# Layer 1's attention with one joint query-key matrix: the normed input takes the place of the keys

## The chip, the cores and the metric

The kernel runs on one core of a Trainium2 chip. The metric is the device time of one execution in microseconds (us). The core has five engines that run side by side and wait for each other by semaphores: PE (TensorE, matmuls and transposes, which writes only to the accumulator memory, PSUM), DVE (VectorE), ACT (ScalarE), POOL (GpSimd) and SP, which issues most of the DMA transfers.

## The reference

The input x is 4 images of 256 channels and 32 x 32 = 1024 positions. Layer 0 is a block of state-space scans, convolutions and an eight-headed attention; it ends in x. Layer 1 treats the positions as tokens t of 256 channels: one attention with a single head of width 256, then a mixture of 16 experts of which each token uses two. All is in 32-bit floats. The part that the change touches:

```
t = _to_tokens(x)
t = t + _L1_attn_ref(_ln_t(t), Wq, bq, Wk, bk, Wv, bv)
t = t + _L1_ffn_ref(_ln_t(t), gate_w, gate_b, w1, w2, w3)

def _L1_attn_ref(traj, Wq, bq, Wk, bk, Wv, bv):
    q = jnp.einsum('bnd,ed->bne', traj, Wq) + bq
    k = jnp.einsum('bnd,ed->bne', traj, Wk) + bk
    v = jnp.einsum('bnd,ed->bne', traj, Wv) + bv
    scores = jnp.einsum('bnd,bmd->bnm', q, k)
    attn = jax.nn.softmax(scores, axis=-1)
    return jnp.einsum('bnm,bmd->bnd', attn, v)
```

A constant that is added to all scores of one query leaves the softmax as it is. With y for the normed token, the score of query n and key m is (Wq y_n + bq) . (Wk y_m + bk); the part with bk is such a constant, so y_m . (Wk^T Wq y_n + Wk^T bq) gives the same attention.

## The kernel before

The work is in stages along the time axis: layer 0's selective scan (about 0 to 1090 us), layer 0's attention for images 0 to 3, one after another (some 1160 to 2247 us), layer 1's attention for the same four images (about 2279 to 2726 us), and the experts with the final addition (to the end).

From layer 0's attention on, the order of every engine's instructions is not written out but computed, before the kernel is compiled, by the class `Plan`. Each step is handed to `add` with its engine, an assumed cost in ns, the keys of what it reads and writes, and the PSUM banks that it takes or gives back. `run` then picks, step by step, what can start first. There are three classes of steps. The main steps are the attention's tiles; each score tile carries a position (n in layer 0, 128 + i in layer 1). The side steps are given by `beside(first, last)`, which spreads the steps of a group evenly over the positions from first to last; such a step is not taken before its position is reached. The third class, low, holds the experts. There are four free PSUM banks (512 columns each); main steps may hold three of them at a time, side steps two, low steps one, and later two. A step that takes two banks waits until it can have both.

Side groups that matter here: `prepare` (line 939) runs in layer 0's attention for image 0, positions 4 to 20. It folds weights: `bias` (L947) multiplies a weight matrix by a bias column, `fold` (L955) multiplies two 256 x 256 matrices into two banks, and DVE copies the product back over the weight (L958). Beside it runs `ahead_of(1)` (line 983), which prepares image 1 for layer 0's attention, at positions 1 to 27. `after_of(b)` (line 1200) finishes layer 0 for an image; for the last one it runs at the start of layer 1's attention (convolution on DVE L1273, mean L1280).

`l1_before(b)` (line 1347) is layer 1's prologue for image b. For image 0 it is spread over positions 17 to 27 of layer 0's last image, for image b + 1 over five positions from the second score tile of image b. It subtracts the mean (`centred`, L1334 on PE, L1338 on DVE) into the buffer `ln`, normalises it in place (`normalised`: squares on ACT L1171, variance on PE L1176, roots on ACT L1182 and L1183, three DVE steps L1186 to L1192, and a multiply by POOL L1196), then projects queries and keys (`matmuls`, L936, evicted from PSUM by ACT with the bias, L1360), and values (L1371, evicted by DVE, L1375). The weights wq, wk and wv are loaded at the start of the kernel (L536).

`l1_attention(i)` (line 1380) handles tile i, 128 queries of image i // 8: scores against all 1024 keys (L1389), their maximum on DVE (L1392), exponentials on ACT (L1396), transposes of these (L1407), and, two tiles later, the weighted sum of the values (L1424). `l1_after(b, half)` (line 1442) runs for each half image: the second norm into the buffer `ln2`, logits of the router (L1458), the choice of two experts on DVE (L1472 to L1489), ranks (L1497) and the scatter of the routing table by POOL (L1531).

The buffers of all this have homes in a table, `homes` (L1315). A pair (s, j) is one of the four buffers of set s that layer 0's attention used; "e", "f", "g" are parts of the transposed exponentials' buffers. The experts later place their weights in set 0, set 1 and a scratch tile, and other things in "e" and "g".

Of the kernel before, what the change touches and what calls it, by code (L numbers as in the profile page):

```python
# [12 lines left out]
AF = mybir.ActivationFunctionType  # L13
# [7 lines left out]
P = 128  # L21
# [38 lines left out]
def _pack(i):  # L60

    f = {k.removeprefix("L0_conv_").removeprefix("L1_attn_").removeprefix("L1_ffn_"): np.asarray(v) for k, v in i.items()}
    f["skip_scale"] = np.asarray(i["L0_conv_skip_scale"])

    def ch(a):

        a = a.reshape(a.shape[0] // P, P, -1)
        return a.transpose(1, 0, 2).reshape(P, -1)

    def cols(a):  # L70

        return np.ascontiguousarray(a.reshape(a.shape[0] // P, P, -1).transpose(1, 0, 2))

    qdw_b = np.zeros((P, 1), np.float32)
    qdw_b[32 : 32 + NB, 0] = f["qdw_b"]
    vec = {
        "norm_w": ch(f["norm_w"]), "norm_b": ch(f["norm_b"]),
        "skip": np.broadcast_to(f["skip_scale"], (P, 1)),
        "qdw_b": qdw_b, "qpw_b": ch(np.repeat(f["qpw_b"], DM)),
        "rdw_w": ch(f["rdw_w"]), "rdw_b": ch(f["rdw_b"]), "rpw_b": ch(f["rpw_b"]),  # L80
        "fdw_w": ch(f["fdw_w"]), "fdw_b": ch(f["fdw_b"]), "fpw_b": ch(f["fpw_b"]),
        "lc_w": ch(f["lc_w"]), "lc_b": ch(f["lc_b"]), "inb": ch(f["attn_inb"]),
        "outb": ch(f["attn_outb"]), "lgn_w": ch(f["lgn_w"]), "lgn_b": ch(f["lgn_b"]),
        "fc_b": ch(f["fc_b"]), "dwc_w": ch(f["dwc_w"]), "dwc_b": ch(f["dwc_b"]),
        "proj_b": ch(f["proj_b"]), "bq": ch(f["bq"]), "bk": ch(f["bk"]),
        "convb": f["m_convb"].T,
        "dtb": f["m_dtb"].T, "dd": f["m_d"].T,

        "alog": f["m_alog"].reshape(NB, DIN // DB, DB, DS).transpose(3, 2, 0, 1).reshape(P, -1),
    }  # L90

    qdw, qpw = np.zeros((C, 3, 32), np.float32), np.zeros((3, 32, C), np.float32)
    for n in range(NB):
        qdw[n * DM : (n + 1) * DM, :, n] = f["qdw_w"][n]
    qpw[:, :NB] = np.repeat(f["qpw_w"][:, :, 0], DM, axis=0).T
    w = {
        "x": f["x"].reshape(B, C, N),
        "vec": np.concatenate([vec[n] for n, _ in _VEC], axis=1),
        "rows": np.concatenate([f["attn_inb"][2 * C :], f["bv"], f["gate_b"]])[None, :],
        "m_in": cols(f["m_inw"].transpose(0, 2, 1).reshape(NB * DM, 2 * DIN)),  # L100

        "convr": np.repeat(f["m_convw"].transpose(0, 2, 1).reshape(CT, 2, 1, K * DIN), DM, axis=2)
        .reshape(CT, P, K, DIN).transpose(1, 0, 2, 3),
        "m_xp": f["m_xpw"][:, :DTR].transpose(1, 0, 2),
        "m_bc": np.repeat(f["m_xpw"][:, DTR:], DB, axis=1).transpose(2, 0, 1),
        "m_dt": f["m_dtw"].transpose(2, 0, 1),
        "m_out": f["m_outw"].transpose(2, 0, 1),
        "qdw": cols(qdw.reshape(C, 96)),
        "qpw": qpw.reshape(96, C),
        "rpw": cols(f["rpw_w"][:, :, 0].T), "fpw": cols(f["fpw_w"][:, :, 0].T),  # L110
        "inw": cols(f["attn_inw"].T), "outw": cols(f["attn_outw"]),
        "fcw": cols(f["fc_w"].T), "projw": cols(f["proj_w"].T),
        "wq": cols(f["Wq"].T), "wk": cols(f["Wk"].T), "wv": cols(f["Wv"].T),
        "gw": cols(f["gate_w"]),

        "we": np.concatenate(
            [
                f[n].reshape(NE, f[n].shape[1] // P, P, -1).transpose(0, 2, 1, 3).reshape(NE * P, -1)
                for n in ("w1", "w2", "w3")
            ],  # L120
            axis=1,
        ),
    }

    strip = np.zeros((P, 2 * P - DB), np.float32)
    strip[np.arange(P), P - DB + np.arange(P) % DB] = 1.0

    pick = np.zeros((3, 32 // DB, DB, 32 // DB, DS, DB), np.float32)  # L130
    for j in range(32 // DB):
        for i in range(DB):
            pick[:, j, i, j, :, i] = 1.0
    grp = np.kron(np.eye(16, dtype=np.float32), np.full((8, 8), 1.0 / (8 * N), np.float32))
    w["const"] = np.concatenate(
        [
            np.eye(P, dtype=np.float32), grp, np.full((P, P), 1.0 / C, np.float32),
            np.broadcast_to(np.arange(NE, dtype=np.float32), (P, NE)),
            np.triu(np.ones((P, P), np.float32), 1), np.ones((P, P), np.float32),
            2.0 * np.arange(TT * P, dtype=np.float32).reshape(TT, P).T,  # L140
            np.broadcast_to(np.arange(NTILE, dtype=np.float32), (P, NTILE)),
            np.arange(P, dtype=np.float32)[:, None], strip,
        ],
        axis=1,
    )
    w["pick"] = pick.reshape(96, -1)
    return {k: np.ascontiguousarray(v) for k, v in w.items()}
# [169 lines left out]
def body(tc, g, out):  # L317
# [8 lines left out]
    with pool("const", 1) as cp, pool("dram", 1, space=bass.MemoryType.DRAM) as drp, contextlib.ExitStack() as late:  # L326
# [16 lines left out]
        def V(name, j=0, n=1):  # L343
            return vec[:, VOFF[name] + j : VOFF[name] + j + n]
# [530 lines left out]
        with pool("sets", 1) as wp, pool("work", 1) as kp, pool("ps2", 1, space=PSUM) as ps:  # L875
# [24 lines left out]
            rss = [kp.tile([P, CT, NT, 4], F32, tag=f"rs{i}", name=f"rs{i}") for i in range(2)]  # L900
            sts = [kp.tile([P, 4, CT], F32, tag=f"st{i}", name=f"st{i}") for i in range(2)]
            small = kp.tile([P, 16 + B * CT], F32, tag="small", name="small")
            fcb, projb, inbq, wmean, grb = small[:, 0:2], small[:, 2:4], small[:, 4:6], small[:, 8:12], small[:, 16:]
            S = [ps.tile([P, N], F32, tag=f"s{i}", name=f"s{i}") for i in range(2)]
            plan.banks = [ps.tile([P, 512], F32, tag=f"k{i}", name=f"k{i}") for i in range(4)]

# [32 lines left out]
            def prepare():  # L939
# [39 lines left out]
                add("DVE", 150, lambda: tt(projb, pb.t[:, 0:2], V("proj_b", 0, 2), ALU.add), (), ["projb"], pb, give=True)  # L979
                for k in range(CT):  # L980
                    add("DVE", 250, lambda k=k: ts(projw[:, k], projw[:, k], V("norm_w", k), None, ALU.mult), ["projw"], ["projw"])

            def ahead_of(b):

# [320 lines left out]
            def place(name):  # L1305
# [7 lines left out]
                return mid(s, j), lambda ks=range(CT), hs=range(2): BK(s, j, ks, hs)  # L1313

            homes = [  # L1315
                dict(ln=(0, 2), sq=(0, 1), q=(0, 3), k=(0, 1), v=(0, 0), ln2=(0, 2), sq2="e"),
                dict(ln=(1, 1), sq="f", q=(1, 3), k="f", v="g", ln2=(1, 1), sq2=(1, 0)),
                dict(ln=(0, 1), sq="e", q=(0, 3), k="e", v=(0, 0), ln2=(0, 1), sq2=(0, 2)),
                dict(ln=(1, 2), sq=(1, 0), q=(1, 3), k="f", v=(1, 0), ln2=(1, 2), sq2=(1, 1)),
            ]  # L1320
            homes = [{n: place(x) for n, x in home.items()} for home in homes]
            rows4 = prs[3].rearrange("p (t c) -> p t c", c=C)
# [24 lines left out]
            def l1_before(b):  # L1347

                home = homes[b]
                ln, lk = home["ln"]  # L1350
                centred([X[b][:, k] for k in range(CT)], lambda ks=range(CT), hs=range(2): KX(b, ks, hs), ln, lk, range(2))
                normalised(ln, lk, *home["sq"], prs[2], ("pr", 2), [range(2)])
                for what, w, bias in (("q", wq, "bq"), ("k", wk, "bk")):
                    dst, dk = home[what]
                    for m in range(CT):
                        for h in range(2):
                            bank = plan.bank()
                            matmuls(bank, w, m, ln, h, [lk([k], [h]) for k in range(CT)])
                            add(
                                "ACT", 580, lambda m=m, h=h, dst=dst, bias=bias, bank=bank: act(dst[m][:, HALVES[h]], bank.t, AF.Identity, bias=V(bias, m), scale=1.0),  # L1360
                                (), dk([m], [h]), bank, give=True,
                            )
                tile_v, vk = v_of(b)
                for u in range(NT // 2):
                    bank = plan.bank()

                    def value(u=u, bank=bank):
                        for c in range(2):
                            for k in range(CT):
                                tok = slice((2 * u + c) * P, (2 * u + c + 1) * P)  # L1370
                                mm(bank.t[:, c * C : (c + 1) * C], ln[k][:, tok], wv[:, k, :], start=k == 0, stop=k == CT - 1)  # L1371
                    add("PE", 1720, value, lk(hs=[u // 2]), (), bank, take=True)
                    dst = homes[b]["v"][0][u // 2][:, u % 2 * 2 * C : (u % 2 + 1) * 2 * C].rearrange("p (t c) -> p t c", c=C)
                    add(
                        "DVE", 690, lambda bank=bank, dst=dst: tt(  # L1375
                            dst, bank.t.rearrange("p (t c) -> p t c", c=C), rows[:, C : 2 * C].unsqueeze(1).to_broadcast([P, 2, C]), ALU.add
                        ), (), vk(2 * u), bank, give=True,
                    )

            def l1_attention(i):  # L1380


                if i < B * NT:
                    b, qt = i // NT, i % NT
                    (q, qk), (kk, kkeys) = homes[b]["q"], homes[b]["k"]
                    for h in range(2):
                        def scores(h=h):
                            for k in range(CT):
# [502 lines left out]
```

## Time and profile before

| what | value |
|---|---|
| median of three runs | 3217.78 us (3207.76 to 3220.32) |
| the profiled execution's own time | 3229.72 us |
| its span (first to last instruction) | 3227.9 us |
| granted clock of TensorE, mean | 0.940 |
| PE busy | 2862.9 us, 89% of the span |
| DVE, ACT, POOL busy | 2048.5, 1534.1, 1183.0 us |
| key projection on PE (L936, weight wk) | 64 records, mean 592 ns, 29.6 us busy |
| query projection on PE (L936, weight wq) | 64 records, mean 736 ns, 37.1 us busy |
| evictions of both (L1360, ACT) | 32, 687 ns each |

A busy share is the time in which an engine carries out at least one instruction. A matmul in 32-bit floats shows as two records, and records of successive matmuls overlap, so that busy time is less than count times mean. "idle before" names the engine whose signal ended a wait. Line numbers are those of the kernel before.

### The profile page before, as it was taken

The numbers are of one execution on the slowest core, as the hardware profiler recorded it, in microseconds if no ns is written. First come the engines' busy times: TensorE is split into PE (matmuls) and PEld (weight loads), VectorE is DVE, ScalarE is ACT, GpSimd is POOL, SyncE is SP. The second block draws the span as 40 slices with busy tenths as digits, with TensorE's granted clock in tenths as the row PEclk, the third lists the DMA queues.
The fourth block names the chain that finished last, engine by engine and source line by source line (L and its number), as shares of the span: only waits on it lengthen the run. The fifth ranks groups of instructions, "written<-read, shape, count | busy, mean of one in ns | idle before, by whom it ended". The sixth has DMA issues, their size and how long they took to land. (4 is left out here: it accounts for less than half of the span.)

```text
span 3227.9 us, 38992 instructions
## 1 busy us (share of the span) xinstructions
PE 2862.9 (89%) x15402; PEld 1616.7 (50%) x15402; DVE 2048.5 (63%) x2336; ACT 1534.1 (48%) x2102; POOL 1183.0 (37%) x747
## 2 busy tenths in 40 slices
PE   6788898988897689999899899988989999799997
PEld 3322222222222145565545555555545666689996
DVE  5899999999999646564865585585364445411112
ACT  3665666566565335455735754665433333211111
POOL 1677777777877400000000010001012123556662
PEclk8899999899999889999999899998989999899998
DMA  3666766676776400000000000000000002355455
GB/s 129 160 169 163 182 168 168 171 177 156 184 175 158 129 0 1 1 1 27 1 1 1 27 1 1 14 1 1 14 1 14 7 14 79 107 148 157 95 125 161
DMA packets 92872, 265.51 MB, mean 82 GB/s; under 512 B 18182, under 2 KB 36086, under 8 KB 89360
## 3 DMA queue, kind: packets, MB, share of 16 engines
q1 hardware_dynamic: 64000, 198.46, 23.2%
q0 software_dynamic: 26512, 60.35, 7.3%
q10 hardware_dynamic: 2176, 4.19, 0.3%
q8 instruction: 122, 2.00, 0.3%
q14 instruction: 62, 0.51, 0.1%
HBM read 291.70 MB, written 42.80 MB: 104 GB/s over the span
## 5 line engine op out<-in xcount | busy, mean ns | idle before, releaser
L841 POOL TENSOR_TENSOR hs<-hs,bc 128x1024 f32<-128x1024 f32 x256 | 603.0, 2357 | 252.1 <-DVE hs L840 235.9
L840 DVE TENSOR_TENSOR_SCAN hs<-dA,dBu 128x1024 f32<-128x1024 f32 x256 | 585.4, 2287 | 30.8 <-DVE dBu L837 1.9
L1106 DVE TENSOR_REDUCE nm<-s 128x1 f32<-128x1024 f32 x256 | 301.5, 1219 | 202.8 <-PE s L1101 201.7
L1111 ACT ACTIVATE pr<-s,nm 128x1024 f32<-128x1024 f32 x256 | 284.8, 1115 | 195.7 <-DVE nm L1106 193.8
L771 ACT ACTIVATE dA<-dA,aneg 128x1024 f32<-128x1024 f32 x256 | 288.9, 1145 | 157.9 <-DMA dA<-ds 148.3
L1125 PE MATMUL k<-const,pr 128*128 128x128 f32 x2048 | 302.1, 291 | 69.3 <-ACT pr L1111 48.3
L1196 POOL TENSOR_TENSOR b<-b,misc 128x1024 f32<-128x1024 f32 x16 | 36.4, 2295 | 892.2 <-DVE misc L1192 663.3
L1125 PEld LDWEIGHTS k<-const,pr 128*128 128x128 f32 x2048 | 234.7, 147 | 188.7 <-issue 82.7
L837 DVE TENSOR_TENSOR dBu<-dBu,bc 128x1024 f32<-128x1024 f32 x256 | 310.0, 1211 | 22.5 <-PE dBu L778 22.4
L1101 PE MATMUL s<-b,b 32*128 32x512 f32 x1024 | 287.7, 650 | 3.3 <-ACT pr L1111 3.3
L778 PE MATMUL dBu<-U,pick 96*128 96x512 bf16 x512 | 161.9, 399 | 123.6 <-DVE hs L840 123.4
L1131 ACT COPY pT<-k 128x512 f32<-128x512 f32 x320 | 175.6, 592 | 173.3 <-PE k L1125 172.2
L789 PE MATMUL pY<-hs,const 128*128 128x512 f32 x512 | 245.0, 601 | 10.8 <-DVE u L481 10.5
L1766 PE MATMUL s<-pT,b 128*128 128x128 f32 x1920 | 230.6, 276 | 3.5 <-DMA b<-we,intse 2.1
L1766 PEld LDWEIGHTS s<-pT,b 128*128 128x128 f32 x1920 | 226.7, 193 | 8.8 <-ACT pT L1769 3.6
L778 PEld LDWEIGHTS <-pick 96*128 96x128 bf16 x512 | 34.7, 98 | 325.9 <-DVE hs L840 206.0
L1770 DVE TENSOR_TENSOR pT<-pT,s 128x512 f32<-128x512 f32 x72 | 49.3, 685 | 229.2 <-ACT pT L1769 177.1
L1131 DVE COPY pT<-k 128x512 f32<-128x512 f32 x192 | 131.5, 686 | 98.8 <-PE k L1125 85.3
L1145 PE MATMUL k<-pT,b 128*32 128x128 f32 x4096 | 153.7, 292 | 17.2 <-DVE pT L1131 14.1
L1145 PEld LDWEIGHTS k<-pT,b 128*32 128x32 f32 x4096 | 114.1, 116 | 73.8 <-issue 30.8
L1101 PEld LDWEIGHTS s<-b,b 32*128 32x128 f32 x1024 | 102.9, 191 | 92.4 <-issue 77.4
L789 PEld LDWEIGHTS pY<-hs,const 128*128 128x128 f32 x512 | 96.5, 191 | 99.3 <-issue 82.3
(441 smaller groups left out, 4649.9 us busy)
## 6 DMA issues: line engine op xcount, KB each, us to landing
dA<-ds SPq DMA_DIRECT2D x256, 512.0 KB, 4.7
dq<-parts SPq DMA_DIRECT2D x15, 768.0 KB, 4.2
U<-dq SPq DMA_DIRECT2D x45, 256.0 KB, 6.0
ds<-dt SPq DMA_DIRECT2D x16, 512.0 KB, 3.0
b<-x SPq DMA_DIRECT2D x4, 1024.0 KB, 7.3
acc<-pr SPq DMA_DIRECT2D x8, 512.0 KB, 7.7
xm<-x SPq DMA_DIRECT2D x4, 1024.0 KB, 5.0
tokens<-pr SPq DMA_DIRECT2D x8, 512.0 KB, 2.9
```

The costliest lines, as they stand in the source:

```text
L771: act(dAs[t], dAs[t], AF.Exp, scale=aneg[:, c : c + 1])
L789: mm(r["pY"][:, h], strip[:, P - DB - j * DB : 2 * P - DB - j * DB], hs[:, h], start=p == 0, stop=p == NJ - 1)
L837: tt(dBu, dBu, r["B"], ALU.mult)
L840: nc.vector.tensor_tensor_scan(hs, dAs.pop(t), dBu, 0.0, ALU.mult, ALU.add)
L841: nc.gpsimd.tensor_tensor(hs, hs, r["C"], ALU.mult)
L1101: mm(S[i][:, HALVES[h]], qT[rr, qt * P : (qt + 1) * P], kT[rr, HALVES[h]], start=True, stop=True)
L1106: "DVE", 1220, lambda i=i, u=u: nc.vector.tensor_reduce(nms[u], S[i], AX.X, ALU.max, negate=True),
L1111: "ACT", 1330, lambda i=i, u=u, hd=hd: act(prs[u % 4], S[i], AF.Exp, bias=nms[u], scale=1.0, accum_out=rss[b % 2][:, k, qt, hd : hd + 1]), ...
L1125: nc.tensor.transpose(bank.t[:, j * P : (j + 1) * P], prs[u][:, c0 : c0 + P], ident)
L1131: lambda dst=dst, bank=bank, on_act=on_act: (nc.scalar.copy if on_act else nc.vector.tensor_copy)(dst, bank.t),
L1145: mm(bank.t[i * HD : (i + 1) * HD, 0:P], v[:, 4 * jh + j, hd * HD : (hd + 1) * HD], pTs[m][jh][:, i, j * P : (j + 1) * P], start=j == 0, s ...
L1766: mm(p12[:, a, c], wbufs[w][:, o : o + P], xT[:, k], start=k == 0, stop=k == CT - 1)
```

## The change

The host hands wq and wk over untransposed. `prepare` gets three steps more, behind its old ones: `q_bias` forms Wk^T bq (four matmuls of one column), `join` forms the joint matrix from wq and wk (four matmuls of 256 columns into two banks), and DVE copies both out of PSUM, the matrix over wq. In the prologue the query projection uses the joint matrix and the new bias; the key projection and its evictions are gone. The scores read `ln` where they read the keys. `ln` must then keep its content until the last score tile of its image, so `ln2`, which used to overwrite it, gets another home, and some homes are exchanged.

```diff
-        "wq": cols(f["Wq"].T), "wk": cols(f["Wk"].T), "wv": cols(f["Wv"].T),
+        "wq": cols(f["Wq"]), "wk": cols(f["Wk"]), "wv": cols(f["Wv"].T),
...
+                qb = plan.bank()
+
+                def q_bias():
+                    for m in range(CT):
+                        for k in range(CT):
+                            mm(qb.t[:, m : m + 1], wk[:, k, m * P : (m + 1) * P], V("bq", k), start=k == 0, stop=k == CT - 1)
+                add("PE", 600, q_bias, ["wq"], (), qb, take=True)
+                add("DVE", 150, lambda: nc.vector.tensor_copy(qbias, qb.t[:, 0:2]), (), ["qbias"], qb, give=True)
+                joint = [plan.bank() for _ in range(CT)]
+
+                def join():
+                    for i in range(CT):
+                        for k in range(CT):
+                            mm(joint[i].t[:, 0:C], wq[:, k, i * P : (i + 1) * P], wk[:, k, :], start=k == 0, stop=k == CT - 1)
+                add("PE", 1800, join, ["wq"], (), joint, take=True)
+                for i in range(CT):
+                    add("DVE", 400, lambda i=i: nc.vector.tensor_copy(wq[:, i], joint[i].t[:, 0:C]), (), ["wq"], joint[i], give=True)
...
-                dict(ln=(0, 2), sq=(0, 1), q=(0, 3), k=(0, 1), v=(0, 0), ln2=(0, 2), sq2="e"),
-                dict(ln=(1, 1), sq="f", q=(1, 3), k="f", v="g", ln2=(1, 1), sq2=(1, 0)),
-                dict(ln=(0, 1), sq="e", q=(0, 3), k="e", v=(0, 0), ln2=(0, 1), sq2=(0, 2)),
-                dict(ln=(1, 2), sq=(1, 0), q=(1, 3), k="f", v=(1, 0), ln2=(1, 2), sq2=(1, 1)),
+                dict(ln=(0, 2), sq=(0, 1), q=(0, 3), v=(0, 0), ln2=(0, 1), sq2="e"),
+                dict(ln=(1, 1), sq="f", q=(1, 3), v="g", ln2="f", sq2=(1, 0)),
+                dict(ln=(0, 2), sq="e", q=(0, 3), v=(0, 0), ln2="e", sq2=(0, 1)),
+                dict(ln=(1, 2), sq=(1, 0), q=(1, 3), v=(1, 0), ln2="f", sq2=(1, 1)),
...
-                for what, w, bias in (("q", wq, "bq"), ("k", wk, "bk")):
-                    dst, dk = home[what]
...
-                            matmuls(bank, w, m, ln, h, [lk([k], [h]) for k in range(CT)])
+                dst, dk = home["q"]
...
+                        matmuls(bank, wq, m, ln, h, [lk([k], [h]) + ["wq"] for k in range(CT)])
...
+                            "ACT", 580, lambda m=m, h=h, dst=dst, bank=bank: act(dst[m][:, HALVES[h]], bank.t, AF.Identity, bias=qbias[:, m : m + 1], scale=1.0),
+                            ["qbias"], dk([m], [h]), bank, give=True,
...
-                    (q, qk), (kk, kkeys) = homes[b]["q"], homes[b]["k"]
+                    (q, qk), (kk, kkeys) = homes[b]["q"], homes[b]["ln"]
```

More of the change, by code (lines that the diff above doesn't have):

```diff
@@ L902, in body @@
             small = kp.tile([P, 16 + B * CT], F32, tag="small", name="small")
-            fcb, projb, inbq, wmean, grb = small[:, 0:2], small[:, 2:4], small[:, 4:6], small[:, 8:12], small[:, 16:]
+            fcb, projb, inbq, qbias, wmean, grb = small[:, 0:2], small[:, 2:4], small[:, 4:6], small[:, 6:8], small[:, 8:12], small[:, 16:]
             S = [ps.tile([P, N], F32, tag=f"s{i}", name=f"s{i}") for i in range(2)]
@@ L1352, in l1_before @@
                 normalised(ln, lk, *home["sq"], prs[2], ("pr", 2), [range(2)])
-                for what, w, bias in (("q", wq, "bq"), ("k", wk, "bk")):
-                    dst, dk = home[what]
-                    for m in range(CT):
-                        for h in range(2):
-                            bank = plan.bank()
-                            matmuls(bank, w, m, ln, h, [lk([k], [h]) for k in range(CT)])
[L1359 to L1362, printed above, removed]
+                dst, dk = home["q"]
+                for m in range(CT):
+                    for h in range(2):
+                        bank = plan.bank()
+                        matmuls(bank, wq, m, ln, h, [lk([k], [h]) + ["wq"] for k in range(CT)])
+                        add(
+                            "ACT", 580, lambda m=m, h=h, dst=dst, bank=bank: act(dst[m][:, HALVES[h]], bank.t, AF.Identity, bias=qbias[:, m : m + 1], scale=1.0),
+                            ["qbias"], dk([m], [h]), bank, give=True,
+                        )
                 tile_v, vk = v_of(b)
```

## The prediction, made before the result was known

> **What bounds the kernel now.** I read the page's busy shares first, then the busy time by stretch of the span, then TensorE's waits in layer 1's attention, and last TensorE's own timeline where the removed work stands.
>
> The first two rows of the page say that TensorE (PE) is the fullest engine over the whole span and that it is nearly full in the second half (the right half of the digits, mostly 9).
>
> ```profile
> PE 2862.9 (89%) x15402; PEld 1616.7 (50%) x15402; DVE 2048.5 (63%) x2336; ACT 1534.1 (48%) x2102; POOL 1183.0 (37%) x747
> ...
> PE   6788898988897689999899899988989999799997
> ```
>
> A mean is not enough, since layer 0's scan (0 to 1090 us) has other limits. The busy times by stretch, cut at the borders of the batches, are these (columns: stretch, length, PE, weight loads, DVE, ACT, POOL, then granted clock):
>
> ```profile
> 1160.00:1457.00 297.00, 274.22 (x2153) 161.10 (x2153) 164.91 (x194) 154.24 (x279) 3.95 (x2) 0.95 0.00 1
> ...
> 2247.00:2279.00 32.00, 26.21 (x131) 15.55 (x130) 6.56 (x9) 9.76 (x15) 4.29 (x2) 0.89 0.00 1
> 2279.00:2361.00 82.00, 81.76 (x312) 50.16 (x311) 43.33 (x62) 36.21 (x51) 4.67 (x2) 1.00 0.04 13
> 2361.00:2395.00 34.00, 23.03 (x57) 11.20 (x58) 24.25 (x28) 16.48 (x19) 5.64 (x2) 0.82 0.00 0
> 2395.00:2425.00 30.00, 30.00 (x90) 16.68 (x88) 9.76 (x12) 7.25 (x10) 7.10 (x5) 0.92 0.00 1
> 2425.00:2508.00 83.00, 77.64 (x297) 48.71 (x298) 40.48 (x107) 28.48 (x43) 24.25 (x35) 0.96 0.05 14
> 2508.00:2621.00 113.00, 108.14 (x438) 70.50 (x437) 53.23 (x130) 38.80 (x58) 26.54 (x38) 0.98 0.03 10
> 2621.00:2726.00 105.00, 100.99 (x438) 68.72 (x437) 54.90 (x160) 34.62 (x53) 24.93 (x39) 1.00 0.11 26
> ```
>
> Layer 1's attention is the stretch from 2279 to about 2726 us. There PE is 94 to 100% busy, except for 34 us from 2361 to 2395; DVE and ACT are about half idle. It is bound by the amount of PE work, so PE work taken out of it should come off the time. In batch 0 of layer 0's attention (1160 to 1457) PE is 92% busy; work put there costs nearly its own length.
>
> The waits of PE from 2247 to 2726 us, in total, are short (columns: us in total, times, longest):
>
> ```profile
> PE k L1497 <- DVE rsum L1428: 8.9, 3, 4.4
> PE k L936 <- POOL b L1196: 5.9, 4, 2.5
> PE k L1280 <- DVE b L1273: 4.4, 1, 4.4
> ```
>
> The timeline of PE at the seam between the layers shows the removed work in place:
>
> ```profile
> 2257.98 7.24 PE L936 MATMUL k<-b,wq 128*128 128x512 f32 x14 [0.36 <-POOL b L1196]
> 2265.06 7.03 PE L936 MATMUL k<-b,wk 128*128 128x512 f32 x16
> 2271.93 7.07 PE L1371 MATMUL k<-wv,b 128*128 128x256 f32 x32
> 2278.83 1.88 PE L1389 MATMUL s<-b,b 128*128 128x512 f32 x4
> ```
>
> The key projection (wk) starts as soon as the query projection ends, and values and scores follow it without a gap. Nothing waits beside it: it is 2271.93 - 2265.06 = 6.87 us of the path.
>
> **What the Trainium skill says.** "Perfetto Trace Analysis", Identifying the Most-Contended Engine: busy matmul time is a poor measure of distance to the roofline because matmuls are pipelined. I use it only to see whether PE ever stands still, and take costs from start to start, not from mean duration: the 16 records of wk have a mean of 592 ns each, which would be 9.5 us, but take 6.87. "TensorE: Matmul & The Clock Gate", The HAM clock gate: PE falls to half clock after an idle window of about 3.4 us. The trace agrees: in the stretch with the 4.36 us wait the clock granted is 0.82, and a wq record that has a median of 592 ns takes up to 1222. "GPSIMD Engine Reference", Specifications: GpSimd shares SBUF interfaces with VectorE and contends with DVE instructions that have two SBUF inputs. The trace agrees: L1474, a subtraction of 64 columns, has a median of 225 ns and takes 2192 beside the POOL multiply of L1196.
>
> **The change part by part.**
>
> Durations of the nearest rows (the sources' own views; min/median/max):
>
> ```profile
> L936 PE MATMUL k<-b,wk x64: 590/592/595, 2265.1 to 2623.9; 128*128 128x512 f32 x64
> L947 PE MATMUL k<-vec,fcw x8: 250/250/271, 1206.6 to 1207.4; 128*128 128x1 f32 x8
> L955 PE MATMUL k<-fcw,outw x8: 379/379/483, 1239.5 to 1241.2; 128*128 128x256 f32 x8
> L958 DVE COPY fcw<-k x2: 415/416/417, 1242.7 to 1259.3; 128x256 f32<-128x256 f32 x2
> ```
>
> Removed from PE: the key projection, 8 matmuls of 512 columns (16 records) per batch, 6.87 us. In batch 0 it is one block; in batches 1 to 3 it is four pieces of 1.72 us (2410.03 to 2411.75 is one), again 6.87 us. PE shows no idle time from 2394 to 2425, nor from 2491 to 2525 and from 2605 to 2640 where the others stand. Sum 4 x 6.87 = 27.5 us, all on the path.
>
> Removed from ACT: 16 evictions (L1360, 687 ns) = 11.0 us. ACT is about half idle there, and scores come after the value projection, so they hid under PE. I count 0. Were ACT the bound they would be worth up to 11.0.
>
> Added to PE, once, in prepare during batch 0 of layer 0: the bias q_bias has the shapes of L947, from 1206.58 to the next instruction at 1207.50 = 0.92 us. The product join has the shapes of L955, 1239.54 to 1241.46 = 1.92 us. Sum 2.8 us. At 92% busy I count it in full; its bounds are 0 (it falls into the 18.3 us that PE waits there for ACT's exponentials, L1111) and about 5. The upper end is the hold of banks: side work may hold two of the four banks at a time and join takes both. Of its twin's two copies, one came at 1242.7 and one at 1259.3, so one bank was out for 17 us; in that time PE waited 0.79 + 0.79 us. So 2.8 plus about 2.
>
> Added to DVE: two copies of 416 ns and one of about 150 (L949, 148 ns) = 1.0 us, where DVE is busy 165 of 297 us. I count 0; without that cover it is 1.0.
>
> Waits that are added: the query matmuls wait for the new wq and their evictions for qbias. Both are made before about 1400 us and used from 2256 us, so behind them nothing stands. No DMA is issued, removed or moved; the key weights are loaded as before, and no instruction of SP or POOL is moved past another by hand.
>
> Moved: buffers. Batch 0's ln stays in its place until its eighth score tile (about 2355 us); its next owner is batch 2's ln, whose first mean is at 2433 us: 78 us to spare. Batch 1's ln place passes to batch 3's second-norm squares two batches later. The second norm takes places that the squares or the keys had. The experts wait for places "e", "g" and the whole of set 0, and these are last read by the second norm of batch 2 either way. I count 0, bounds 0 and 2 us.
>
> Moved: the plan. The order on every queue is computed from costs and positions, and layer 1's prologue now has 32 steps in place of 40 over the same five positions, so its POOL multiplies fall due about half a position later (5 x 15/32 - 5 x 15/40 = 0.47; batch 1's eight score tiles take from 2425.5 to 2536, 13.8 us each, so about 6 us). At 2256 and 2391 us the query projection waits for that multiply, which had been due long before; in batches 2 and 3 it stands two score tiles ahead of its own first scores (2491 against 2536 us). I count 0. What can move is the meeting of POOL's multiply with the routing steps of L1474 to L1489, which today costs PE the three waits of L1497, 8.9 us. A new plan can lose them (-8.9) or make one in each of the other five halves (5 x 4.4 = +22).
>
> What is late next: after the keys are gone, PE's own rest, 94 to 100% busy. In the 34 us from 2361 PE waits for the tail of batch 3 of layer 0 on DVE (L1273) and the normalisation chain. That chain starts at 2278 us (L1204), directly behind the value evictions, so it comes 6.87 us earlier with them, and the wait keeps its length.
>
> Sum: -27.5 + 2.8 = -24.7 us. The profiled execution took 3229.72 us (span 3227.9): 3205.0. It lies 11.94 us above the median of the three runs, 3217.78 (3207.76 to 3220.32), so in those terms 3193.1, or -0.77%.
>
> **The rivals.** About 0.5% (16 us) is what a measurement of this kernel can tell from no change.
>
> A, the forecast: all four projections come off, 3193. For it: no PE gap at any of them. Chance 0.60.
>
> B, only half comes off. If the tail chain at 2361 does not start earlier with the seam, batch 0's 6.87 us becomes wait there; and one more meeting with POOL eats about 4.4: -24.7 + 6.9 + 4.4 = -13.4, 3204. For it: that stretch is the one place where DVE's chain and not PE sets the end. Against it: the chain's first step stands right behind the value evictions. Chance 0.24.
>
> C, more comes off: the three L1497 waits go as well, -24.7 - 8.9 = -33.6, 3184. For it: two of them come from POOL's multiply starting in the very microsecond in which the routing steps start, and that multiply now falls due later. Chance 0.09.
>
> D, slower. Place: join in batch 0 of layer 0. While it waits for two free side banks and holds them, the preparation of batch 1 behind it stands still. Its last PE step today ends about 1393 us and batch 1 begins about 1457, so 64 us are spare. The hold decides only from there: to be slower by 16 us it would have to last 64 + 24.7 + 16 = 105 us. A hold of 110 us gives 3239. Against it: the twin held for 17 us. Chance 0.07.
>
> That the keys' work is not really removed can't be: scores read ln in place of k, and no other step makes k.
>
> **How the numbers follow.** Likeliest: 3193. A spreads by some 8 us, since three runs of one kernel spread over 12.6. Of A about 0.53 is beyond 16 us, with C's 0.09 and 0.04 of B: faster 0.66. Same: the rest of A and B, 0.27. Slower: 0.07. The range leaves out D and the outer tails: from 3177 (C less 7) to 3214 (B and 10 of spread).
>
> **What would show it.** Right: no wk rows; PE busy in all lower by about 25 us; the value projection directly behind the query projection at the seam; the distance from the first layer 1 score to the end of the last one shorter by about 20 us, with waits of PE as long as before. Two small groups for the join near 1200 to 1400 us. Wrong: the start of layer 1 later than before by more than 3 us (D or a worse plan of layer 0); longer waits of PE in 2247 to 2726, with L1497 or L936 <- POOL (B); or the wait at L1280 grown by 6.9 us.

## The result and the profile after

The changed kernel takes 3189.95 us (median of six runs, 3184.59 to 3197.09). Six runs of the kernel before give 3214.79 (3207.76 to 3220.32). The difference of the medians is 24.8 us. The ratio is 0.993, with a 95% interval of 0.9919 to 0.9942: 0.6 to 0.8% faster. The forecast was 3193.

The page of the kernel after shows PE with 39 us less to do than before. Its place as the fullest engine and the digits of the second half have hardly changed:

```profile
PE 2824.0 (89%) x15354; PEld 1598.7 (50%) x15354; DVE 2047.2 (64%) x2339; ACT 1522.3 (48%) x2086; POOL 1183.4 (37%) x747
...
PE   6788888898888779999899889989989999899996
```

The busy times by stretch, with PE's in the third column: image 0 of layer 0's attention; the seam up to the first score of layer 1; to the first score of image 1; to the first query projection of image 2; to that of image 3; to the last score. The last cuts lie earlier in their images than those of the prediction's table, so these rows can't be compared with that table one by one:

```profile
1160.00:1457.00 297.00, 271.43 (x2136) 158.66 (x2134) 164.75 (x196) 152.59 (x276) 3.95 (x2) 0.95 0.00 1
2242.00:2268.00 26.00, 20.12 (x119) 12.87 (x118) 6.33 (x9) 7.45 (x11) 4.29 (x2) 0.80 0.00 1
2268.00:2405.00 137.00, 125.96 (x432) 72.73 (x431) 76.25 (x102) 57.90 (x76) 17.60 (x9) 0.94 0.02 8
2405.00:2472.00 67.00, 62.76 (x266) 41.85 (x264) 37.99 (x94) 23.97 (x35) 15.50 (x20) 1.00 0.06 16
2472.00:2579.00 107.00, 102.14 (x425) 68.45 (x425) 53.50 (x134) 36.04 (x53) 26.54 (x38) 0.98 0.04 11
2579.00:2697.00 118.00, 111.44 (x464) 74.38 (x465) 57.29 (x171) 36.12 (x55) 34.68 (x55) 0.96 0.11 27
```

Over the whole of layer 1's attention with its seam, PE was busy 447.77 of 479 us before and is busy 422.42 of 455 now. So 25.4 us of work are gone, while the idle time stayed (31.2 and 32.6 us). The waits of PE in that window (us in total, times, longest) are the same ones with nearly the same lengths, except for one on a DMA:

```profile
PE k L1516 <- DVE rsum L1447: 8.5, 3, 4.0
PE k L936 <- POOL b L1216: 5.8, 3, 2.9
PE k L1708 <- DMA misc<-table,tcole: 5.5, 1, 5.5
PE k L1300 <- DVE b L1293: 4.4, 1, 4.4
```

(L1516, L1447, L1216, L1300 and L1293 are L1497, L1428, L1196, L1280 and L1273 of the kernel before.) L1708, L1689 before, belongs to the experts, which begin beside the last scores. In this profile of the kernel before PE waited there for only 1.2 us:

```profile
PE k L1689 <- DMA misc<-table,tcole: 1.2, 1, 1.2
```

In a second profile of the same kernel (before_again, below) it waited 5.3 us, so the longer wait is not the change's.

At the seam the timeline of PE shows what filled the removed block's place: the value projection now follows the query projection directly.

```profile
2251.90 9.80 PE L936 MATMUL k<-b,wq 128*128 128x512 f32 x16 [2.93 <-POOL b L1216]
2261.54 7.07 PE L1390 MATMUL k<-wv,b 128*128 128x256 f32 x32
2268.44 1.88 PE L1408 MATMUL s<-b 128*128 128x512 f32 x4
```

The added steps stand in layer 0's image 0, in order the bias product, the joint product and its two copies:

```profile
L990 PE MATMUL k<-vec,wk x8: 250/250/271, 1302.0 to 1302.8; 128*128 128x1 f32 x8
```

```profile
L998 PE MATMUL k<-wk,wq x8: 379/379/483, 1323.8 to 1325.4; 128*128 128x256 f32 x8
L1001 DVE COPY wq<-k x2: 414/415/416, 1330.0 to 1340.2; 128x256 f32<-128x256 f32 x2
```

The two first profiles differ by 43.1 us (spans of 3227.9 and 3184.8), which is more than the medians do. By stage, from the first score of layer 0 to the first query projection, from there to the start of the last score record of layer 1, and from there to the end of the span:

| kernel | layer 0's attention | layer 1's attention | experts and end |
|---|---|---|---|
| before | 1080.5 | 470.1 | 501.8 |
| after | 1075.9 | 444.5 | 488.4 |
| difference | -4.6 | -25.6 | -13.4 |

Only the middle column holds the removed work; of the change, the first holds the small added steps and the last nothing. The experiments look at the outer ones. Within the middle column, the time falls at every image (from the first query projection to the first score of image 0, then from first score to first score, then to the last score; before_again is the second profile of the kernel before):

| kernel | seam | image 0 | image 1 | image 2 | image 3 |
|---|---|---|---|---|---|
| before | 22.8 | 146.7 | 110.4 | 113.0 | 77.2 |
| before_again | 22.8 | 146.6 | 110.4 | 113.0 | 80.8 |
| after | 16.6 | 136.9 | 104.2 | 106.1 | 80.7 |

An image's projection runs beside the image ahead of it, so the four blocks lie in the first four columns, and each column lost 6 to 10 us. The last column holds the wait on the DMA.

### The profile page after: what moved, and what is told of

It reads as the page before. It is cut to its first block, busy times and chain, and to the rows that moved or that the text cites. A ratio compares the mean times of both kernels' runs of the same rounds, so it can differ in the third digit from the quotient of the medians.

```text
span 3184.8 us, 38887 instructions
## 1 busy us (share of the span) xinstructions
PE 2824.0 (89%) x15354; PEld 1598.7 (50%) x15354; DVE 2047.2 (64%) x2339; ACT 1522.3 (48%) x2086; POOL 1183.4 (37%) x747
## 5 line engine op out<-in xcount | busy, mean ns | idle before, releaser
L1216 POOL TENSOR_TENSOR b<-b,misc 128x1024 f32<-128x1024 f32 x16 | 36.4, 2299 | 887.5 <-DVE misc L1212 835.4
L837 DVE TENSOR_TENSOR dBu<-dBu,bc 128x1024 f32<-128x1024 f32 x256 | 310.0, 1211 | 19.9 <-PE dBu L778 19.8
```

What stands on the lines that cost most here:

```text
L837: tt(dBu, dBu, r["B"], ALU.mult)
```

## The experiments

**First question: is it the removed PE work, or something that went with it?** Three kernels add parts of the key projection back to the changed kernel as dead work, so their outputs are unchanged. `keys_back` adds all of it:

```diff
+                for m in range(CT):
+                    for h in range(2):
+                        bank = plan.bank()
+                        matmuls(bank, wk, m, ln, h, [lk([k], [h]) for k in range(CT)])
+                        add("ACT", 580, lambda m=m, bank=bank: act(kx, bank.t, AF.Identity, bias=V("bk", m), scale=1.0), (), ["kx"], bank, give=True)
```

> The changed kernel with the key projection added again as dead work: the same 8 matmuls of 512 columns per image with the key weights (32 in all) and the same 16 evictions by ACT, into a scratch tile that nobody reads; scores still read the normed input. Theory work (what counts is PE work taken from a full PE): all four projections cost their start-to-start time again, 4 x 6.87 = 27.5, so 3189.95 + 27.5 = 3217.5 us, about 2.7 slower than the kernel before (the join is still there). Theory plan (the gain came from a luckier order of the queues, since the whole plan is computed anew): the time stays near 3190 or lands anywhere, not at +27. Theory half (only the seam and one image's block count): about 3204.

`keys_pe_only` keeps the matmuls and gives the bank back without an eviction:

```diff
+                        matmuls(bank, wk, m, ln, h, [lk([k], [h]) for k in range(CT)])
+                        bank.ops[-1]["give"] = True
```

> The changed kernel with only the PE half of the key projection added again: 32 matmuls of 512 columns into a PSUM bank that is given back at once; no eviction, no ACT work. Theory work: 3217.5, the same as with evictions, since these hid under PE. Theory ACT (the evictions or the time for which a bank is held were what was removed): clearly less, at most half of the 27.5, 3204 or below.

`evict_only` adds only ACT instructions:

```diff
+                        add("ACT", 580, lambda m=m, h=h, dst=dst: act(kx, dst[m][:, HALVES[h]], AF.Identity, bias=V("bk", m), scale=1.0), dk([m], [h]), ["kx"])
```

> The changed kernel with 16 ACT instructions of 512 columns added, each a second pass over a query tile into a scratch tile that nobody reads, so ACT has as much to do as with the key evictions (16 x 0.687 = 11.0 us) and PE has no more. Theory work: within 2 us of 3190. Theory ACT: +11, 3201.

They ran on a chip where the kernel before takes 3227.13 us, so they are compared by ratio to it:

| kernel | median us | ratio to before | 95% interval |
|---|---|---|---|
| changed kernel (first measurement) | 3189.95 | 0.993 | 0.9919 to 0.9942 |
| keys_back | 3228.65 | 1.0008 | 0.9998 to 1.0018 |
| keys_pe_only | 3230.02 | 1.001 | 0.9998 to 1.0021 |
| evict_only | 3203.93 | 0.9924 | 0.9909 to 0.994 |

The matmuls alone bring back 1.001 / 0.993 = 0.8%, some 26 us of 3190; the two intervals together leave about 5 us either way. With the evictions it is no more. The evictions alone change nothing that can be measured. All three kernels keep the new homes of the buffers and an order that is computed anew, so neither of these is the gain either. It is the PE work, and ACT's 11 us hid under it. The profile of keys_pe_only has the key projection's 64 records, and layer 1's attention takes 474.1 us again (2258.3 to 2732.4):

```profile
L936 PE MATMUL k<-b,wk x64: 590/592/593, 2267.9 to 2622.1; 128*128 128x512 f32 x64
```

**Second question: what does the preparation cost?** `join_only` adds the new steps to the kernel before, with their results in scratch tiles:

```diff
+                add("PE", 600, q_bias, ["wq"], (), qb, take=True)
+                add("DVE", 150, lambda: nc.vector.tensor_copy(qbias, qb.t[:, 0:2]), (), ["qbias"], qb, give=True)
...
+                add("PE", 1800, join, ["wq"], (), joint, take=True)
+                for i in range(CT):
+                    add("DVE", 400, lambda i=i: nc.vector.tensor_copy(jt[:, i], joint[i].t[:, 0:C]), (), ["jt"], joint[i], give=True)
```

> The kernel before with only the new steps of the preparation added: the bias product, the joint product into two banks, and the three copies by DVE, into scratch tiles that nobody reads; queries and keys are projected as before. Theory work: +2.8 (bounds 0 and 5), 3217.6 against 3214.8. Theory plan: a shift of up to 10 us in either direction, since the plan of layer 0 is computed anew. Theory bank hold: +5 or more, with waits of PE between the join and its second copy.

Measured 3230.57, ratio 1.0011 (0.9998 to 1.0024): +3.5 us, with an interval from -0.6 to +7.7. The estimate of 2.8 lies within it, and so does nothing at all; the price is not settled more closely than that.

`join_one_bank` asks whether the two banks matter. On the changed kernel both halves go into one bank:

```diff
-                joint = [plan.bank() for _ in range(CT)]
+                joint = plan.bank()
...
-                            mm(joint[i].t[:, 0:C], wq[:, k, i * P : (i + 1) * P], wk[:, k, :], start=k == 0, stop=k == CT - 1)
+                            mm(joint.t[:, i * C : (i + 1) * C], wq[:, k, i * P : (i + 1) * P], wk[:, k, :], start=k == 0, stop=k == CT - 1)
```

> The changed kernel with both halves of the joint product put into one PSUM bank of 512 columns and copied by one DVE instruction, so that the step takes one side bank in place of two. Theory work: the work is the same, within 2 us of 3190. Theory bank hold: faster by what PE lost between the join and its second copy, up to 5 us, 3185.

Measured 3202.88 where before takes 3227.58: 0.9922 (0.9908 to 0.9937). That is 2.6 us less than 0.993, and the intervals overlap almost wholly: no effect shown.

**Third question: does the plan, computed anew, give or take anything?** `dues_40` fills each prologue up to 40 steps with empty ones, so that all its steps fall due where they did before:

```diff
+                for _ in range(8):
+                    add("SP", 0, lambda: None)
```

> The changed kernel with eight empty steps in each prologue (on SP's list, no instruction comes of them), so that its other steps fall due at the positions they had in the kernel before. Theory due times don't bind: within 3 us of 3190. Theory due times (a prologue that falls due half a position later makes PE wait at the seams): faster than 3190, up to 6 per image, 3166 at most.

Measured 3201.91, ratio 0.993 (0.9912 to 0.9948), the same as the changed kernel. In the traces PE, DVE and POOL keep exactly the order that they have in the changed kernel, and on ACT one square moves ahead of two copies; layer 1's stage takes 445.0 us (444.5 in the changed kernel). So the due times do not bind. The run says nothing of what another order of PE would cost.

**Fourth question: where is the wait of the query projection from, and what is it worth?** `mult_dve` takes the changed kernel and puts the prologue's two closing multiplies on DVE:

```diff
-                normalised(ln, lk, *home["sq"], prs[2], ("pr", 2), [range(2)])
+                normalised(ln, lk, *home["sq"], prs[2], ("pr", 2), [range(2)], last=True)
```

> The changed kernel with the two multiplies that end the prologue's normalisation put on DVE in place of POOL, as the last half image has them already. Theory meeting (the routing steps on DVE are slowed where POOL's multiply runs beside them, and PE waits for them and for the multiply): the waits of PE on POOL at L936 (5.8 us) and most of those at L1516 on L1447 (8.0 in two images) go, in exchange for 1.2 us DVE each; 6 to 12 faster, 3178 to 3184. Theory DVE full (the tail of layer 0 needs DVE at the first seam): no gain or slower, 3190 to 3195.

Measured 3188.76 where before takes 3227.58: 0.9885 (0.9867 to 0.9902). Against 0.993 this is another 14.5 us, with some 7 us of uncertainty either way; 6 to 12 were expected. The routing step that POOL's multiply slowed is L1493 (L1474 in the kernel before), 64 columns on DVE. Here it is in the changed kernel, with its three durations being the shortest, the median and the longest:

```profile
L1493 DVE TENSOR_TENSOR gpr<-gpr,m x8: 224/226/2187, 2404.3 to 2733.7; 128x64 f32<-128x64 f32 x8
```

And here with the multiply on DVE:

```profile
L1493 DVE TENSOR_TENSOR gpr<-gpr,m x8: 224/224/226, 2399.9 to 2731.8; 128x64 f32<-128x64 f32 x8
```

The longest fell from 2187 to 226 ns. The waits of PE at L1516 on L1447 fell from 8.5 to 4.2 us, but the wait of the query projection hardly did; the multiply is now DVE's and still late at image 1:

```profile
PE k L936 <- DVE b L1216: 5.4, 2, 3.7
...
PE k L1516 <- DVE rsum L1447: 4.2, 5, 1.4
```

Layer 1's stage fell by 10.7 us (444.5 to 433.8), and PE's idle time in it by only 4.5 (26.7 to 22.2). The rest is in PE's busy time, 417.8 against 411.6 us for the same instructions, at a mean granted clock of 0.96 against 0.98. It is lost in the work that follows a wait. The query projection of image 2 in the changed kernel, after a wait of 3.98 us:

```profile
2471.11 0.41 PE L1516 MATMUL k<-oh,const 128*128 128x64 f32 x2 [3.98 <-DVE rsum L1447]
...
2472.34 8.68 PE L936 MATMUL k<-b,wq 128*128 128x512 f32 x16
```

The same with the multiply on DVE, after 1.41 us:

```profile
2464.56 0.41 PE L1516 MATMUL k<-oh,const 128*128 128x64 f32 x2 [1.41 <-DVE rsum L1447]
...
2467.64 7.03 PE L936 MATMUL k<-b,wq 128*128 128x512 f32 x16
```

The same sixteen records take 8.68 us after the long wait and 7.03 after the short one. The granted clock tells why: it is 0.50 from 2472.2 to 2475.4 us in the changed kernel, and 1.00 from 2464.6 to 2474.6 us here.

`before_mult_dve` makes that one edit on the kernel before, and `mult_all_dve` makes it on the changed kernel for the second norm as well:

```diff
-                normalised(ln, lk, *home["sq2"], prs[2], ("pr", 2), [[half]], last=(b, half) == (B - 1, 1))
+                normalised(ln, lk, *home["sq2"], prs[2], ("pr", 2), [[half]], last=True)
```

> The kernel before with the two multiplies that end the prologue's normalisation on DVE in place of POOL. Theory meeting: what the multiply costs is independent of the keys, so the gain is that of the same step on the changed kernel, 0.9885 against 0.993, some 14 us: ratio 0.995 to 0.996. Theory freed DVE (it pays only because the joint matrix gave the seam room): under 5 us.

> The changed kernel with every normalising multiply of layer 1 on DVE: the prologue's and those of the second norm's half images (14 of 512 columns per image pair go from POOL's 1.23 us each to about 0.65). Theory meeting: only multiplies that run beside the routing steps cost; those of the second norm come before them, so little more than with the prologue's alone: ratio 0.987 to 0.989. Theory DVE full: slower than that, 0.990 or more.

Beside 3214.99 for the kernel before, before_mult_dve takes 3201.05, 0.9959 (0.9946 to 0.9972): 13.2 us off, about as much as on the changed kernel. So what this multiply costs was there before, and the change neither made nor removed it. mult_all_dve, which moves 14 multiplies in all beyond those of mult_dve, takes 3176.37, 0.9878 (0.9863 to 0.9892), the fastest of all, though not to be told from mult_dve's 0.9885.

**Fifth question: what are the outer columns of the stage table?** `before_again` and `after_again` are the two kernels unchanged.

> The kernel before, unchanged, profiled once more. Its first profiled execution lay 15 us above the median of its six runs, so the two profiles differ by 43 us where the medians differ by 24.8. Theory work: the stages up to the last score tile of layer 1 repeat within 2 us (q start at 2256, last score tile at about 2725), and the excess lies in the experts' stage, which then takes some 490 in place of 503 us. Theory plan: nothing differs, since the plan is the same, and the time is near 3230 again.

> The changed kernel, unchanged, beside the kernel before on one chip. Theory work: ratio 0.992 to 0.994; in the profile the stage from the first query projection to the last score tile takes 445 to 448 us, and the stages around it (layer 0's attention, the experts) repeat those of the kernel before, 1080 and 501 us, so that the extra 18 us of the first pair of profiles (43 in place of 25) are chance. Theory plan: the stages around it are shorter again (1076 and 488).

before_again took 3232.65 us, in one run only, and after_again 3191.2 (0.9929, 0.9917 to 0.9941). All stages from the profiles:

| kernel | before's median beside it | layer 0 | layer 1 | experts and end |
|---|---|---|---|---|
| before_again | 3227.58 | 1080.6 | 473.6 | 500.6 |
| join_only | 3227.13 | 1079.3 | 473.7 | 496.9 |
| keys_back | 3227.13 | 1080.3 | 473.2 | 500.6 |
| keys_pe_only | 3227.13 | 1086.1 | 474.1 | 503.8 |
| evict_only | 3227.13 | 1086.1 | 447.9 | 501.5 |
| dues_40 | 3227.58 | 1080.3 | 445.0 | 500.3 |
| join_one_bank | 3227.58 | 1080.4 | 446.5 | 501.8 |
| mult_dve | 3227.58 | 1074.6 | 433.8 | 503.2 |
| before_mult_dve | 3214.99 | 1079.4 | 459.0 | 488.0 |
| mult_all_dve | 3214.99 | 1079.3 | 431.4 | 489.6 |
| after_again | 3214.99 | 1075.8 | 447.3 | 489.3 |

Both expectations failed in a part. before_again did not lose the excess: its experts again take about 501 us. Its layer 1 did not repeat within 2 us either, but is 3.5 us longer, since the wait of L1689 on the DMA is 5.3 us in place of 1.2. after_again repeated the short outer stages that I had called chance.

The experts' stage goes with the chip or the session: it takes 488 to 490 us in every run beside a before of 3215 and 497 to 504 in every run beside one of 3227, with or without keys. The later runs were on one chip in the first case and on two others in the second, each in one session, so chip and session can't be told apart, and why the stage is longer was not sought. PE's waits for DMAs in it are no guide: 22.6 us in after_again, 19.8 in dues_40. The first profile of before, with 501.8, fits in as well: its execution of 3229.72 us stands in the record among the eleven runs of before with the median 3227.58, and not among the six beside the changed kernel. So the first two profiles come from different chips or sessions, and the 13.4 us between their experts' stages are not the change's.

Layer 0's 1075.9 repeats for the changed kernel, while dues_40, with the same order of PE there, takes 1080.3. The difference is in PE's busy time for the same instructions, 979.3 against 984.2 us. The clock goes with it: summed over the stage, the trace's clock records withhold 52.0 us from PE in the changed kernel, 56.3 in dues_40 and 60.6 in keys_pe_only, whose stage takes 1086.1. What sets this amount from kernel to kernel stays open.

In layer 1's column, five profiles with the key projection and POOL's multiply (the kernel before, before_again, join_only, keys_back, keys_pe_only) lie between 470.1 and 474.1, mean 472.9. Five without keys (the kernel after, after_again, evict_only, dues_40, join_one_bank) lie between 444.5 and 447.9, mean 446.2. The difference is 26.7 us, without overlap. (The wait on the experts' DMA is in it, on average 4.3 us with keys and 6.2 without; leaving it out, the difference is 28.6.)

## Why the prediction was right

The forecast was -24.7 us; the medians moved by -24.8. Agreement to 0.1 us is luck, for the interval of the ratio allows 18.6 to 26.0 us; but that interval leaves out the 13.4 of rival B, the 33.6 of rival C and a slower kernel (D). The distance from the first score of layer 1 to the last fell from 447.3 to 427.9 us, by the 20 or so that were named as a sign. Term by term:

- Key projection off PE, 27.5 expected: 26.7 between the means of five and five profiles, and some 26 from adding the matmuls back. All four images' blocks came off the path (the table by image), so rival B, with half of them, is out.
- Evictions off ACT, 0 expected: evict_only and keys_pe_only both show it.
- The join, 2.8 expected: 3.5 measured, with -0.6 to 7.7 around it. The right size, but not a sharp test; near-equal totals here do not prove each small term.
- DVE's copies and the buffers kept longer, 0 expected: layer 1 shows no wait of PE that the kernel before does not have in one of its two profiles, or at nearly the same length.
- The tail of layer 0 (the wait at L1300) was to move along with the seam and keep its length. It did: 4.36 us before and after. Its chain started 10.4 us earlier (the reciprocal at the head, L1204 before and L1224 after, went from 2278.0 to 2267.6). Of these, 4.1 us are the earlier start of the whole stage (2256.0 to 2251.9); the other 6.3 are near the 6.87 of the removed block.
- The plan, 0 expected: the later due times cost nothing in dues_40. keys_back and keys_pe_only, planned anew as well, come back to the time before.
- Rival D, the hold of banks: the joint product's second copy came 16 us after its matmuls began, where its twin's came 20 us after (1239.5 to 1259.3; the prediction's 17 is the time between the twin's two copies, which is 10 here), and image 0 of layer 0 ended at 1457.8 in place of 1457.4. It was nowhere near the 105 us from which it would have decided.
- Rival C, the loss of the L1497 waits, did not happen; these waits stayed at 8.5 us. Its price was too small: removing the cause (mult_dve) brought 14.5 us in the timing and 10.7 in the stage, where I had put 8.9 for the waits alone, of which only 4.3 went. What I left out is that PE works more slowly for some us after a wait of 4. I had the clock of 0.82 behind such a wait in front of me, but gave it no price.
- One announced sign was wrong: PE's busy time in all fell by 38.9 us and not by 25. Layer 1 gave 25.4 of it. The experts' stage gave 5.0 (450.1 to 445.2) and layer 0's attention 7.8 (987.2 to 979.4), where nothing was removed. A busy sum mixes in the granted clock (0.940 against 0.943 over the span). In these two stages the clock records withhold 4.8 us (23.2 to 18.4) and 6.0 us (58.0 to 52.0) less than before, about what the sums lost there.
- The 11.94 us that the prediction took for one slow execution are in the main a difference of chip or session, as the experts' stage shows. It did not touch the forecast, which is a difference.

## What to carry to other kernels

Where one engine is busy for 94 to 100% of a stage, price a removed step from start to start in the timeline, not as count times mean: here 6.87 us and not 9.5 an image, and the sum held. Two matrices that are only ever applied one after the other can be multiplied once; the price is one product of the weights, the gain a projection per image, and the buffer that stands in has to live longer, which cost nothing that can be seen here, where its next owner comes later anyway. Compare stages rather than spans when two profiles come from different runs: 18 of the 43 us between these two were in stages that the change hardly touches.

## What the runs showed of the hardware that was not expected

A wait of PE can cost more than its length. Sixteen records that take 7.03 us after a wait of 1.41 took 8.68 after one of 3.98. The page "TensorE: Matmul & The Clock Gate" of the Trainium skill (The HAM clock gate) says that the clock falls after an idle window of about 3.4 us. The runs agree that it falls, and give the price here as 1.65 us on top of a wait of 4. They differ in the length: in the changed kernel, after 7 us of full clock, a single wait of 2.88 us was enough (the last three numbers of the second line are granted clock, DMA share and GB/s):

```profile
2376.57 2.07 PE L1196 MATMUL k<-pT,const 128*128 128x512 f32 x2 [2.88 <-DVE pT L1209]
2376.60:2379.80 3.20, 3.20 (x4) 1.15 (x4) 2.03 (x3) 2.85 (x3) 1.28 (x1) 0.50 0.00 0
```

After the wait of 1.41 us in mult_dve the clock stayed at 1.00. Where between the two it begins to fall was not tried.

A small DVE instruction can be held up tenfold by a POOL instruction beside it: 64 columns took 2187 ns in place of 226 while POOL multiplied 1024-column tiles, and 226 at most once that multiply was gone. Which instructions are held up shows in the changed kernel beside the two multiplies of image 3:

```profile
2569.45 4.34 POOL L1216 TENSOR_TENSOR b<-b,pr 128x1024 f32<-128x1024 f32 x2 [16.71 <-DVE gpr L1491]
2569.73 2.19 DVE L1493 TENSOR_TENSOR gpr<-gpr,m 128x64 f32<-128x64 f32 x1
2572.24 0.22 DVE L1498 TENSOR_REDUCE sm<-gpr 128x4 f32<-128x64 f32 x1 [0.32 <-ACT gpr L1495]
2572.49 0.18 DVE L1499 RECIPROCAL sm<-sm 128x4 f32<-128x4 f32 x1
2572.71 1.17 DVE L1500 TENSOR_TENSOR gpr<-gpr,sm 128x64 f32<-128x64 f32 x1
```

The two that read two tiles (L1493, L1500; 226 and 225 ns in the median) end only when a multiply of POOL is over: the second ends at 2573.88 us, POOL at 2573.79. The reduction and the reciprocal, which read one, take their usual 220 and 178 ns beside the second multiply.

The same kernel, with the same data, took 3215 us on one chip and 3227 on two others, each in one session. The profiles beside these runs differ by about as much in the experts' stage.
